# Wide input matmuls in a GRU, a new order of the opening, and a last attention batch whose logits follow head by head

## The chip, the core and the metric

The kernel runs on one core of one Trainium2 chip, in float32 throughout. The metric is the device time of one execution in microseconds. Engines are named as in the profile: PE is TensorE's matmul (PEld its weight load), DVE is VectorE, ACT is ScalarE, POOL is GpSimd, SP is SyncE, which issues most of the transfers.

## What is computed

`x` is (16, 256, 512) and `cond` is (16, 512). First an attention block with an adaptive norm is added to `x`, then a GRU runs over the 256 time steps of the result, with `cond` as its first state, and its states are added too.

```python
scale, shift = split(cond @ W_emb + b_emb)               # per batch
xn  = rms_norm(x, g_norm) * (1 + scale) + shift
q, k, v = heads(xn @ W_qkv)                              # 16 heads of 32
q, k = rms_norm(q, g_q), rms_norm(k, g_k)
o   = softmax(q k^T * 32**-0.5) v
x   = x + (o + o @ W_out)
# GRU over time, h = cond at t = 0
gi, gh = x_t @ W_ih + b_ih, h @ W_hh + b_hh
r, z = sigmoid(gi_r + gh_r), sigmoid(gi_z + gh_z)
n    = tanh(gi_n + r * gh_n)
h    = (1 - z) * n + z * h
out  = x + h
```

## The kernel before

**Attention.** The batches are worked one after the other. For each batch `project` (L246) makes q, k and v of two halves of 128 tokens in units of one half, one of q, k and v, and one of four chunks `k` of the contraction. `turn_qk` and `put_qk` bring q and k into `qT` and `kT`, with the heads on the partitions. The 16 heads are four groups of four. A group has its logits (`logits`, L314; four heads of 32 rows side by side in the array, one PSUM bank `lg0` to `lg3` each), their maxima (`maxima`, DVE, L330), exponentials with sums (`exps`, ACT, L336), a reciprocal (DVE, L344) and a scaling (`normalize`, POOL, L347). The weights are then turned by PE (`turn_pair`, L220, two heads at a time into two banks each), copied to SBUF (`put_turned_bank`, L376, DVE or ACT), multiplied with v (`weigh`, L393) and copied into `oT` (`put_weighed`, L404). `slot0` to `slot3` are the four groups of a batch. They mix the attention of batch b with the projections of batch b + 1, so PE has work while the other engines make the softmax. `last_batch` has no next batch to mix in: there the turn of a group stands in the slot of the group after it, and its `weigh` one slot later still.

**Opening.** The weights arrive while batch 0 is normed. `rows` holds `b_emb` and `g_norm`, and is turned into columns by PE. `g_q`, `g_k` and a second layout of `cond` (`rows_b`, `cond_p`) are loaded by SP after `x` of batch 1 and turned by PE just before q and k are turned (L674, L675). The biases of the GRU follow on SP (L129 to L131). `Stats` and `norm_qk` norm q and k from PSUM.

**GRU.** `h` is kept turned, hidden units on the partitions. A gate's PSUM tile has 32 partitions for each quarter of 128 units, 16 batches for each of two steps: a pair of steps shares its tiles, and two pairs alternate. Each product is four matmuls, one for each quarter, in four column tiles of the array. `gate_part` (L803) adds one chunk of the contraction. `input_part` adds the input's share for both steps of a pair at once, 128 columns for each of the gates r, n and z. `state_part` adds the state's share for one step. The tile of n has two blocks, the input's share and the state's, since r multiplies only the second. `open_gate` writes the biases by matmuls the first time, and `seed` by ACT copies later. In each step PE does the state's products (three gates, four chunks), then one step of `output_step` (`oT @ W_out` for a later block of 16 steps, 256 columns), then half of the next pair's input products (`parts[6 * s : 6 * s + 6]`). Meanwhile DVE turns the gates (`turned`, L827), ACT makes r, n and z, DVE makes h (L935 to L937), and POOL adds the result to `x`. `project_first` makes the `W_out` products of the first 16 steps within the last batch, chunk k from group k.

**Order.** Under `manual_schedule` the engines PE, DVE, ACT and POOL take their instructions in the written order. SP is not among them: its transfers go when their buffers are free and its queue comes to them.

Of the kernel before, what the change touches and what calls it, by code (L numbers as in the profile page):

```python
# [19 lines left out]
def kernel(  # L20
# [69 lines left out]

    rows = p1.tile([12, P], F32, tag="qkn", name="rows", bufs=4)
    nc.scalar.dma_start(rows[0:8, :], b_emb.rearrange("(m c) -> m c", c=P))
    nc.scalar.dma_start(rows[8:12, :], g_norm.rearrange("(m c) -> m c", c=P))
    x_tiles = {}
# [15 lines left out]
    rows_b = p1.tile([2, P], F32, tag="qkn", name="rows_b", bufs=4)  # L110
    cond_p = p1.tile([KC * B, P], F32, tag="qkn", name="cond_p", bufs=4)
    b_more = p1.tile([P, 2, P], F32, name="b_more")
    for r, g in ((0, g_q), (1, g_k)):
        nc.sync.dma_start(
            rows_b[r : r + 1, :].rearrange("o (i d) -> o i d", d=DH),
            g.rearrange("(o i d) -> o i d", o=1, i=1).to_broadcast([1, HG, DH]),
        )
    for k in range(KC):
        nc.sync.dma_start(
            cond_p[k * B : (k + 1) * B, :].rearrange("b (j c) -> b j c", c=32),  # L120
            cond.rearrange("b (j k c) -> k b j c", k=KC, c=32)[k],
        )
    for j in range(4):
        bi, bh = (
            b.rearrange("(o g j f) -> j o g f", o=1, g=3, f=P)[j].to_broadcast([32, 3, P])
            for b in (b_ih, b_hh)
        )
        r = slice(32 * j, 32 * j + 32)
        nc.sync.dma_start(b_rows[r, 0:3, :], bi)  # L129
        nc.sync.dma_start(b_rows[r, 3, :], bh[:, 2, :])  # L130
        nc.sync.dma_start(b_more[r], bh[:, 0:2, :])  # L131
# [172 lines left out]
    def logits(b, g):  # L304

        w = Group()
        w.b, w.g = b, g
        w.lg = [
            ps_lg.tile([P, NT, T], F32, tag=f"lg{i}", name=f"lg_{b}_{g}_{i}") for i in range(HG)
        ]  # L310
        for n in range(NT):
            for i in range(HG):
                r = slice(i * DH, (i + 1) * DH)
                nc.tensor.matmul(  # L314
                    w.lg[i][:, n, :],
                    qT[r, g, n * P : (n + 1) * P],
                    kT[r, g, :],
                    start=True,
                    stop=True,
                )  # L320
        w.turned = []
        w.neg = small.tile([P, HG, NT], F32, tag="neg", name=f"neg_{b}_{g}")
        w.den = small.tile([P, HG, NT], F32, tag="den", name=f"den_{b}_{g}")
        w.rden = small.tile([P, HG, NT], F32, tag="rden", name=f"rden_{b}_{g}")
        w.attn = [None] * HG
        return w

# [154 lines left out]
    def slot2(b, w, prev, st):  # L482
# [19 lines left out]
        if b == 0:  # L502

            for c in range(KC):
                d = wo[:, c, c * P : (c + 1) * P]
                nc.vector.tensor_tensor(d, d, ident, ALU.add)
        elif b == 1:
            nc.vector.tensor_tensor(b_rows[:, 0:2, :], b_rows[:, 0:2, :], b_more, ALU.add)
# [49 lines left out]

    def last_batch(prev):


        b, before = B - 1, None
        w = logits(b, 0)
        for g in range(NG):
            if before:
                weigh(before, "Z")
            turn_pair(prev, 0, "AX")
            maxima(w, (0, 1))
            exps(w, (0, 1))
            if before:  # L570
                put_weighed(before, nc.vector)
            turn_pair(prev, 1, "YZ")
            maxima(w, (2, 3))
            exps(w, (2, 3))
            put_turned_bank(prev, 0, nc.vector)
            normalize(w, (0, 1))
            put_turned_bank(prev, 2, nc.vector)
            put_turned_bank(prev, 1, nc.scalar)
            put_turned_bank(prev, 3, nc.scalar)
            if g < NG - 1:  # L580
                normalize(w, (2, 3))
                before, prev, w = prev, w, logits(b, g + 1)
        project_first(0)
# [3 lines left out]
        turn_pair(w, 0, ("lg2", "lg3"))  # L587
        turn_pair(w, 1, "AX")
        weigh(prev, "Z")
        put_turned(w, "vava")  # L590
        put_weighed(prev)
        weigh(w, "Y")
        put_weighed(w, nc.vector)
        project_first(2)
        project_first(3)

# [3 lines left out]
    with tc.manual_schedule(engines=ORDERED):  # L600
# [17 lines left out]
        tp = tile_ps("tp_rows", "A")  # L618
        nc.tensor.transpose(tp[:, :12], rows, ident[:12, :12])
        nc.vector.tensor_copy(cols[:, :12], tp[:, :12])  # L620
        for k in range(KC):
            for j in range(4):
# [9 lines left out]
        norm_apply(0, batches[0].rs.second())  # L632
        load_x(2)
# [19 lines left out]
        for k in range(KC):  # L653
            for n in range(NT):
                for i in range(2):
                    accs[n][i] = project(0, n, i, (k,), accs[n][i])
        v = project(0, 0, 2, range(KC), "lg0")
        norm_first(1)
        batches[1].rs.first()
        norm_apply(1, batches[1].rs.second())  # L660
        s0, s1 = Stats(0, 0), Stats(0, 1)
        s0.add(0, s0.square(0, accs[0][0]))
        s0.add(1, s0.square(1, accs[0][1]))
        sq = s1.square(0, accs[1][0])
        s0.rs.first()
        s1.add(0, sq)
        sq = s1.square(1, accs[1][1])
        rstd = s0.rs.second()
        s1.add(1, sq)
        s1.rs.first()  # L670
        qk0 = norm_qk(0, 0, accs[0], rstd)
        qk1 = norm_qk(0, 1, accs[1], s1.rs.second())
        tp = tile_ps("tp_rows_b", "lg1")
        nc.tensor.transpose(tp[:, :2], rows_b, ident[:2, :2])  # L674
        nc.tensor.transpose(tp[:, 64 : 64 + KC * B], cond_p, ident[: KC * B, : KC * B])  # L675
# [4 lines left out]
        norm_first(2)  # L680
        nc.vector.tensor_copy(cols[:, 12:], tp[:, :2])
        nc.vector.tensor_scalar(gq_col, cols[:, 12:13], DH ** -0.5, None, ALU.mult)
        nc.vector.tensor_copy(gk_col, cols[:, 13:14])
        nc.vector.tensor_copy(h0P.rearrange("p k b -> p (k b)"), tp[:, 64 : 64 + KC * B])
# [6 lines left out]
        for b in range(B - 1):  # L691
            for g in range(NG):
                w = logits(b, g)
                (slot0, slot1, slot2, slot3)[g](b, w, prev, st)
                prev = w
        last_batch(prev)

    TG = P // B  # L700
    xins = {}

    def in_blocks(a, i, j, s):

        a = a[:, i * TG : (i + 1) * TG, :].rearrange("b (s i) (j f) -> s j b i f", s=2, f=P)
        return a[s, j]

    def load_block(i):
        if i < T // TG:
            xins[i] = xin.tile([P, TG // 2, KC, 32], F32, tag="xin", name=f"xin_{i}")  # L710
            for j in range(4):
                for s in range(2):
                    r = 32 * j + B * s
                    nc.sync.dma_start(
                        xins[i][r : r + B].rearrange("b i q c -> b i (q c)"), in_blocks(x, i, j, s)
                    )

    for i in range(4):
        load_block(i)


    whh = wpool.tile([P, KC, 3 * D], F32, tag="w_b", name="whh")
    load_rows(whh, w_hh)
# [7 lines left out]

    R_, Z_, N_ = range(3)
    gates = [
        [tile_ps(f"g{name}_{i}", banks[i], (P, w, P)) for i in range(2)]
        for name, banks, w in (("r", ("A", "lg2"), 1), ("z", ("X", "lg3"), 1), ("n", "ZY", 2))
    ]
# [42 lines left out]
    def open_gate(p, g):  # L781

        for i in range(gates[g][p].shape[1]):
            for j in range(4):
                nc.tensor.matmul(
                    gates[g][p][32 * j : 32 * j + 32, i, :],
                    ident[:, 32 * j : 32 * j + 32],
                    b_rows[:, g + i, :],

                    start=(i == 0),  # L790
                    stop=True,
                    skip_group_check=True,
                )

    def seed(p):

        nc.scalar.copy(gates[R_][p % 2][:, 0, :], b_rows[:, 0, :])
        nc.scalar.copy(gates[N_][p % 2], b_rows[:, 2:4, :])
        nc.scalar.copy(gates[Z_][p % 2][:, 0, :], b_rows[:, 1, :])

    def gate_part(dst, rows, w, g, k, stationary):
        for j in range(4):
            nc.tensor.matmul(  # L803
                dst[32 * j : 32 * j + rows, :],
                stationary,
                w[:, k, g * D + P * j : g * D + P * j + P],
                start=False,
                stop=True,
                skip_group_check=True,
            )  # L810

    def input_part(p, g, k):
# [3 lines left out]
        gate_part(gates[g][p % 2][:, 0, :], 32, wih, g, k, x2)  # L816

    def state_part(t, g, hT):

        dst = gates[g][t // 2 % 2]  # L820
        for k in range(KC):
            gate_part(dst[:, dst.shape[1] - 1, :], hT.shape[2], whh, g, k, hT[:, k, :])
# [42 lines left out]
    with tc.manual_schedule(engines=ORDERED):  # L865
# [11 lines left out]
        for g in (R_, N_, Z_):  # L877
            open_gate(0, g)
            state_part(0, g, h0P)
            for k in range(KC):  # L880
                input_part(0, g, k)
        parts = [(g, k) for g in (R_, N_, Z_) for k in range(KC)]
# [104 lines left out]
```

## Time and profile before

| | us |
|---|---|
| median of 3 timed runs | 1752.92 (1748.24 to 1756.32) |
| profiled execution, its own time | 1767.2 |
| its span, first to last instruction | 1765.4 |
| opening, to the first logits | 0 to 35.79 |
| attention of batches 0 to 14 | 35.79 to 586.39 |
| last batch and the GRU's step 0 | 586.39 to 630.64 |
| GRU from step 1 | 630.64 to 1765.4 |

PE busy is 99% of the span, PEld 78%, DVE 60%, ACT 42%, POOL 18%. The mean granted clock of PE is 0.995. In a timeline row the figures are the start in us, the length of the merged stretch, the engine, the line, the operation, and the number of records (x32). Each float32 matmul shows as two records ("passes"), each with its own weight load. In a row of waits the figures are us in total, how often, and the longest. In a row of windows they are the stretch, its length, the busy time of PE, PEld, DVE, ACT and POOL, the granted clock (PEclk), the share of the DMA engines and GB/s.

### The profile page before, as it was taken

The page shows a single profiled execution, that of the slowest core. Times are in us where ns is not written, and L with a number is a line of the kernel's source. Part 1 is how long each engine was busy: PE and PEld are TensorE (multiplying, and loading weights), DVE is VectorE, ACT ScalarE, POOL GpSimd, SP SyncE. Part 2 cuts the span into 40 slices and gives each one's busy share as a digit, 9 for nine tenths or more (in the row PEclk, how much of TensorE's full clock was granted, in tenths as well). Part 3 has the DMA queues.
Part 4 walks back from the last instruction along what each step waited for, and adds up shares of the span by engine and source line. Part 5 has one row for each costly group of instructions (what it writes and reads, how often), then busy time and mean ns, then how long its engine had stood idle before and what let it go on. Part 6 is the DMA issues. An engine that isn't in the chain of part 4 may idle for free.

```text
span 1752.9 us, 103866 instructions
## 1 busy us (share of the span) xinstructions
PE 1734.2 (99%) x46980; PEld 1375.6 (78%) x46980; DVE 1055.3 (60%) x3313; ACT 740.9 (42%) x2694; POOL 315.6 (18%) x773
## 2 busy tenths in 40 slices
PE   8999999999999999999999999999999999999998
PEld 4444444444444589999999999999999999999997
DVE  4777777777776755555555555555555555555554
ACT  4777877787777722222222222222222222222222
POOL 0433444334433500000000000000000000000000
PEclk9999999999999999999999999999999999999999
DMA  7300000000000310000000100000001000000000
GB/s 247 78 14 14 14 26 14 14 14 14 14 2 2 74 28 22 17 17 23 23 17 16 23 23 17 17 23 23 17 17 22 23 17 17 17 10 11 11 17 16
DMA packets 49962, 44.90 MB, mean 26 GB/s; under 512 B 9619, under 2 KB 42751, under 8 KB 49519
## 3 DMA queue, kind: packets, MB, share of 16 engines
q1 hardware_dynamic: 49399, 38.21, 8.3%
q8 instruction: 368, 6.03, 1.5%
q14 instruction: 75, 0.61, 0.1%
q10 hardware_dynamic: 120, 0.04, 0.0%
HBM read 29.83 MB, written 8.39 MB: 22 GB/s over the span
## 4 chain that ended last, share of the span: by engine, by line
PE 97%; DVE 1%; ACT 1%; issue 1%; DMA 0%; SPq 0%; DVEq 0%; ACTq 0%
PE qkv L246 20%; PE gr L803 19%; PE gn L803 19%; PE gz L803 19%; PE o L747 6%; PE lg L314 4%; PE tpa L220 4%; PE o L393 4%; PE tpqk L220 1%; ACT attn L336 1%; PE tpx L220 1%; DMA we<-in_L_cond_W_emb_dram 0%; PE first L549 0%; DVE trh L827 0%; ACT n L908 0%
## 5 line engine op out<-in xcount | busy, mean ns | idle before, releaser
L246 PE MATMUL qkv<-wq,xnT 128*32 128x512 f32 x3072 | 355.6, 597 | 1.1 <-DVE xnT L238 1.1
L347 POOL TENSOR_SCALAR attn<-attn,rden 128x256 f32<-128x256 f32 x510 | 232.8, 478 | 378.3 <-DVE rden L344 254.2
L904 ACT ACTIVATE r<-trr 128x64 f32<-128x64 f32 x256 | 65.6, 256 | 521.1 <-DVE trr L827 521.1
L336 ACT ACTIVATE attn<-lg,neg 128x256 f32<-128x256 f32 x512 | 234.4, 483 | 64.0 <-DVE neg L330 46.9
L246 PEld LDWEIGHTS qkv<-wq,xnT 128*32 128x32 f32 x3072 | 88.3, 109 | 183.3 <-issue 158.2
L827 DVE STREAM_TRANSPOSE trr<-gr 128x128 f32<-128x128 f32 x256 | 81.1, 317 | 249.8 <-PE gr L803 249.7
L908 ACT ACTIVATE n<-n 128x64 f32<-128x64 f32 x256 | 65.7, 257 | 309.8 <-DVE n L907 306.9
L330 DVE TENSOR_REDUCE neg<-lg 128x2 f32<-128x512 f32 x256 | 159.2, 683 | 48.2 <-PE lg L314 48.1
L803 PE MATMUL gn<-wih,xT 128*32 128x128 f32 x4096 | 172.1, 273 | 0.1
L827 DVE STREAM_TRANSPOSE trh<-gn 128x128 f32<-128x128 f32 x256 | 81.1, 317 | 143.3 <-PE gn L803 143.3
L747 PE MATMUL o<-oT,wo 128*32 128x256 f32 x1920 | 159.9, 379 | 0.0
L803 PEld LDWEIGHTS gn<-wih,xT 128*32 128x32 f32 x4096 | 136.0, 110 | 12.7 <-issue 0.3
L803 PE MATMUL gr<-whh,padded 128*32 128x128 f32 x4096 | 141.8, 273 | 2.5 <-DVE padded L937 1.7
L803 PE MATMUL gr<-wih,xT 128*32 128x128 f32 x4096 | 142.8, 273 | 0.2
L803 PE MATMUL gz<-wih,xT 128*32 128x128 f32 x4096 | 142.6, 273 | 0.3
L803 PE MATMUL gz<-whh,padded 128*32 128x128 f32 x4096 | 142.1, 273 | 0.0
L803 PE MATMUL gn<-whh,padded 128*32 128x128 f32 x4096 | 141.6, 273 | 0.0
L803 PE MATMUL gr<-whh,h 128*16 128x128 f32 x4064 | 140.5, 273 | 0.4
L803 PE MATMUL gn<-whh,h 128*16 128x128 f32 x4064 | 140.4, 273 | 0.2
L803 PE MATMUL gz<-whh,h 128*16 128x128 f32 x4064 | 140.1, 273 | 0.0
L939 POOL TENSOR_TENSOR y<-xT,padded 128x64 f32<-128x64 f32 x128 | 41.1, 321 | 538.6 <-DVE padded L937 538.6
L803 PEld LDWEIGHTS gr<-wih,xT 128*32 128x32 f32 x4096 | 127.2, 110 | 13.0 <-issue 0.6
(127 smaller groups left out, 2782.0 us busy)
## 6 DMA issues: line engine op xcount, KB each, us to landing
x<-in_x_dram SPq DMA_DIRECT2D x16, 512.0 KB, 3.6
xin<-in_x_dram SPq DMA_DIRECT2D x256, 32.0 KB, 2.8
out_dram<-osb SPq DMA_DIRECT2D x248, 32.0 KB, 2.8
wq<-in_L_cond_W_qkv_dram SPq DMA_DIRECT2D x4, 768.0 KB, 9.9
wih<-in_L_cond_W_ih_dram SPq DMA_DIRECT2D x16, 192.0 KB, 7.0
whh<-in_L_cond_W_hh_dram SPq DMA_DIRECT2D x16, 192.0 KB, 6.7
we<-in_L_cond_W_emb_dram SPq DMA_DIRECT2D x4, 512.0 KB, 6.1
wo<-in_L_cond_W_out_dram SPq DMA_DIRECT2D x1, 1024.0 KB, 10.5
```

The lines of the kernel that those rows point to most:

```text
L220: nc.tensor.transpose(dst[r], src[q], ident[q, q])
L246: nc.tensor.matmul(a[32 * j : 32 * j + 32, :], batches[b].xnT[:, k, n * P + 32 * j : n * P + 32 * j + 32], wq[:, k, s * D : (s + 1) * D], ...
L314: nc.tensor.matmul(w.lg[i][:, n, :], qT[r, g, n * P : (n + 1) * P], kT[r, g, :], start=True, stop=True,)
L330: nc.vector.tensor_reduce(w.neg[:, i, :], w.lg[i], AX.X, ALU.max, negate=True)
L336: nc.scalar.activation(a[:, n, :], w.lg[i][:, n, :], AF.Exp, bias=w.neg[:, i, n : n + 1], accum_out=w.den[:, i, n : n + 1],)
L347: engine.tensor_scalar(w.attn[i][:, n, :], w.attn[i][:, n, :], w.rden[:, i, n : n + 1], 1.0, ALU.mult, ALU.mult,)
L393: nc.tensor.matmul(w.o[i * DH : (i + 1) * DH, :], v[:, k, h * DH : (h + 1) * DH], w.attnT[:, i, k, :], start=(k == 0), stop=(k == NT - 1),)
L747: nc.tensor.matmul(acc[32 * j : 32 * j + 32, :], w[:, k, P * j + 32 * m : P * j + 32 * m + 32], rhs, start=(k == 0), stop=(k == KC - 1),)
L803: nc.tensor.matmul(dst[32 * j : 32 * j + rows, :], stationary, w[:, k, g * D + P * j : g * D + P * j + P], start=False, stop=True, skip_gr ...
L827: nc.vector.transpose(tr.rearrange("p q s b -> p (q s b)"), gate)
L904: nc.scalar.activation(r, turned("r", t, gr[:, 0, :])[:, :, s, :], AF.Sigmoid)
L908: nc.scalar.activation(n, n, AF.Tanh)
```

## The change

It has three parts.

1. **GRU.** The tile of r gets a second block, and the input's share of n goes there. So `input_part` for r is one matmul of 256 columns (r's and n's columns of `W_ih`, two separated blocks of the moving operand) for each quarter and chunk, and z keeps 128 columns. The state's share of n has a tile to itself. `parts` has 8 entries in place of 12, three in the first step of a pair and five in the second. DVE turns the input's share of n after r, not before it. `open_gates` opens tiles with matmuls as wide as the tile.
2. **Opening.** `g_q` and `g_k` come with `rows` on ACT's queue. The units of q and k of batch 0 have a new order, and so have the statistics behind them. The biases and the first state move to `load_small`, issued in `slot2` of batch 0; the first state's second layout is copied from `h0T` by DMA.
3. **Last batch.** The logits of a head are written after the exponentials that free its bank, and its maximum follows them. A group is turned and weighed in one slot. `project_first(0)` moves into the last slot. The openings of step 0's gates and its state products stand between the last turns, `weigh` and `project_first(3)`.

The diff, cut to its core:

```diff
+    def load_small():
+        for j in range(4):
...
+            for i, g in enumerate((0, 2, 1)):
+                nc.sync.dma_start(b_rows[r, i, :], bi[:, g, :])
+            nc.sync.dma_start(b_rows[r, 3, :], bh[:, 2, :])
+            nc.sync.dma_start(b_more[r], bh[:, 0:2, :])
+            for q in range(KC):
+                nc.sync.dma_start(h0P[r, q, :], h0T[32 * q : 32 * q + 32, j, :])
...
+    def add_logits(w, heads):
+        for i in heads:
+            w.lg[i] = ps_lg.tile([P, NT, T], F32, tag=f"lg{i}", name=f"lg_{w.b}_{w.g}_{i}")
+        for n in range(NT):
+            for i in heads:
+                r = slice(i * DH, (i + 1) * DH)
+                nc.tensor.matmul(
+                    w.lg[i][:, n, :],
+                    qT[r, w.g, n * P : (n + 1) * P],
+                    kT[r, w.g, :],
...
-        elif b == 1:
-            nc.vector.tensor_tensor(b_rows[:, 0:2, :], b_rows[:, 0:2, :], b_more, ALU.add)
+            load_small()
+        elif b == 2:
+            for i in range(2):
+                a = b_rows[:, 2 * i, :]
+                nc.vector.tensor_tensor(a, a, b_more[:, i, :], ALU.add)
...
+    def open_gates(p, which=(R_, N_, Z_)):
+        for g, name, bank, row, n in (
+            (R_, "r", ("lg2", "A")[p], 0, 2), (N_, "n", ("lg3", "X")[p], 3, 1),
+            (Z_, "z", "ZY"[p], 2, 1),
+        ):
...
+    def gate_part(dst, rows, w, first, k, stationary):
+        for j in range(4):
+            nc.tensor.matmul(
+                dst[32 * j : 32 * j + rows],
+                stationary,
+                w[:, k, :].rearrange("p (g j c) -> p j g c", g=3, c=P)[:, j, first::2][:, : dst.shape[1]],
...
     def last_batch(prev):
-        b, before = B - 1, None
-        w = logits(b, 0)
+        w = logits(B - 1, 0)
+        maxima(w, range(HG))
         for g in range(NG):
-            if before:
-                weigh(before, "Z")
+            last = g == NG - 1
             turn_pair(prev, 0, "AX")
-            maxima(w, (0, 1))
             exps(w, (0, 1))
-            if before:
-                put_weighed(before, nc.vector)
+            put_turned_bank(prev, 0, nc.vector)
             turn_pair(prev, 1, "YZ")
-            maxima(w, (2, 3))
-            exps(w, (2, 3))
-            put_turned_bank(prev, 0, nc.vector)
+            put_turned_bank(prev, 2, nc.vector)
             normalize(w, (0, 1))
-            put_turned_bank(prev, 2, nc.vector)
             put_turned_bank(prev, 1, nc.scalar)
             put_turned_bank(prev, 3, nc.scalar)
-            if g < NG - 1:
-                normalize(w, (2, 3))
-                before, prev, w = prev, w, logits(b, g + 1)
-        project_first(0)
+            if last:
+                project_first(0)
+            else:
+                after = logits(B - 1, g + 1, ())
+                for i in (0, 1):
+                    add_logits(after, (i,))
+                    maxima(after, (i,))
+            weigh(prev, "Y")
+            exps(w, (2, 3))
+            put_weighed(prev, nc.vector)
+            if last:
+                break
+            normalize(w, (2, 3))
+            for i in (2, 3):
+                add_logits(after, (i,))
+                maxima(after, (i,))
+            prev, w = w, after
         project_first(1)
         normalize(w, (2,), nc.vector)
         normalize(w, (3,))
-        turn_pair(w, 0, ("lg2", "lg3"))
-        turn_pair(w, 1, "AX")
-        weigh(prev, "Z")
-        put_turned(w, "vava")
-        put_weighed(prev)
-        weigh(w, "Y")
+        turn_pair(w, 0, "AX")
+        put_turned_bank(w, 0, nc.vector)
+        put_turned_bank(w, 1, nc.scalar)
+        project_first(2)
+        turn_pair(w, 1, "YZ")
+        put_turned_bank(w, 2, nc.vector)
+        put_turned_bank(w, 3, nc.scalar)
+        open_gates(0, (R_, N_))
+        weigh(w, "A")
         put_weighed(w, nc.vector)
-        project_first(2)
+        open_gates(0, (Z_,))
+        state_part(0, R_, h0P)
         project_first(3)
+        state_part(0, N_, h0P)
+        state_part(0, Z_, h0P)
...
-        for k in range(KC):
-            for n in range(NT):
-                for i in range(2):
-                    accs[n][i] = project(0, n, i, (k,), accs[n][i])
+        for ks, n in (((0,), 0), ((0,), 1), ((1,), 0), ((1,), 1), ((2, 3), 0), ((2, 3), 1)):
+            for i in range(2):
+                accs[n][i] = project(0, n, i, ks, accs[n][i])
...
-        nc.scalar.copy(gates[R_][p % 2][:, 0, :], b_rows[:, 0, :])
-        nc.scalar.copy(gates[N_][p % 2], b_rows[:, 2:4, :])
-        nc.scalar.copy(gates[Z_][p % 2][:, 0, :], b_rows[:, 1, :])
+        nc.scalar.copy(gates[R_, p % 2], b_rows[:, 0:2, :])
+        nc.scalar.copy(gates[N_, p % 2][:, 0, :], b_rows[:, 3, :])
+        nc.scalar.copy(gates[Z_, p % 2][:, 0, :], b_rows[:, 2, :])
...
-        parts = [(g, k) for g in (R_, N_, Z_) for k in range(KC)]
+        parts = [(g, k) for g in (R_, Z_) for k in range(KC)]
...
-            if s == 0:
-                ni = turned("i", t, gn[:, 0, :])
...
             nc.scalar.activation(r, turned("r", t, gr[:, 0, :])[:, :, s, :], AF.Sigmoid)
+            if s == 0:
+                ni = turned("i", t, gr[:, 1, :])
...
-                for g, k in parts[6 * s : 6 * s + 6]:
+                for g, k in (parts[:3], parts[3:])[s]:
                     input_part(p + 1, g, k)
```

The blocks of x for the GRU and `W_hh` are now written before `last_batch` (the blocks first, as they were).

## The prediction

> **What bounds the kernel now.** I read the page first: shares, the chain that ended last, the groups; then the timeline of TensorE (PE) inside the second half, the waits there, and every engine's timeline of the two stretches that the diff reorders (0 to 60 us, 586 to 631 us).
>
> ```profile
> PE 1742.9 (99%) x46980; PEld 1384.4 (78%) x46980; DVE 1054.6 (60%) x3313; ACT 741.4 (42%) x2694; POOL 316.7 (18%) x773
> ...
> PE 96%; DVE 1%; ACT 1%; DMA 1%; issue 1%; SPq 0%; DVEq 0%; ACTq 0%
> ...
> L747 PE MATMUL o<-oT,wo 128*32 128x256 f32 x1920 | 169.9, 379 | 0.9 <-issue 0.8
> ```
>
> PE carries 96% of the chain, so only PE's passes and its stalls count, apart from the ends and the last attention batch. Two steps of the recurrence, in PE's timeline:
>
> ```profile
> 661.78 1.06 PE L803 MATMUL gr<-whh,h 128*16 128x128 f32 x32
> 662.65 1.06 PE L803 MATMUL gn<-whh,h 128*16 128x128 f32 x32
> 663.52 1.06 PE L803 MATMUL gz<-whh,h 128*16 128x128 f32 x32
> ...
> 666.14 1.06 PE L803 MATMUL gr<-whh,padded 128*32 128x128 f32 x32
> ```
>
> A step is 666.14 - 661.78 = 4.36 us. 32 passes take 0.87 us from start to start: eight rounds of four column tiles, 109.1 ns a round of 128 columns. A step has 24 rounds for the state, 12 for the input, two of 256 columns for the output: 36 x 0.1091 = 3.93, so a 256 round takes (4.362 - 3.93)/2 = 0.216 us. The step is PE's own streaming, nothing else. The last 16 steps (no output product) take 4.23 and 4.18 us, with PE waiting for h: that is the recurrence's own chain, 0.13 us below the step.
>
> But some steps are longer. What the weight loads (PEld) waited for in 640 to 1690 us, and two of the places:
>
> ```profile
> PEld gz L803 <- issue: 4.8, 15, 0.5
> PEld gn L803 <- issue: 3.4, 11, 0.3
> PEld o L747 <- issue: 2.8, 7, 0.5
> PEld gr L803 <- issue: 2.8, 8, 0.5
> ```
> ```profile
> 762.65 0.12 PEld L747 LDWEIGHTS o<-oT,wo 128*32 128x32 f32 x3 [0.53 <-issue]
> ```
>
> 13.8 us in 41 stops, waiting for no engine. They stand at 758.6, 762.65, 766.7 us: one block of instructions apart. Counting TensorE's records, every such stop falls on the same place modulo 256, some 1.4 us after a packet of the instruction queue ended (16 KB each). So the instruction stream is late: 304 instructions a step, 256 each 3.67 us.
>
> Last batch, granted clock (PEclk is the third figure from the end):
>
> ```profile
> 590.22:593.63 3.41, 2.87 (x22) 1.55 (x26) 1.99 (x6) 2.85 (x11) 2.82 (x7) 1.00 1.00 222
> 593.63:597.05 3.42, 3.42 (x46) 2.45 (x40) 2.78 (x5) 2.93 (x13) 0.84 (x2) 0.50 1.03 228
> ```
>
> Here PE has gaps, and the clock falls to half for 3.4 us, and again from 603.87 to 610.70.
>
> **The change, part by part.** Sums are against the profiled execution (1767.2 us, span 1765.4). The median of the timed runs, 1752.92, is 14.3 us lower, almost exactly all late fetches (14.2 us over the second half): timed runs must have few of them. I return to this at the end.
>
> *Opening.* Now q and k of batch 0 finish after 13 to 16 of 16 units of 0.86 us; in the new order after 10, 12, 14, 16. DVE's line of statistics starts 2.6 us earlier; the last unit ends where it did (28.7 us). Worked through: second sum of squares 29.7 to 30.35, scale 31.7, q and k of half 1 normalized 31.7 to 32.95 (now 32.33 to 33.62), no wait for gq_col (now 33.54 to 33.93), puts 33.0 to 34.6 (now 33.98 to 35.64). First logits at 34.75 instead of 35.79: -1.0. The value product, ending at 32.06, is then PE's bound. Moved past: SP loses 18 small DMAs (8.0 to 25.6 us), so x of batch 2, W_out and W_ih are issued earlier, behind W_qkv on one queue; nothing waits for them. ACT's queue gets two broadcasts (0.26 to 0.58 each); its first work is at 5.43, waiting for x: hidden. Without that cover 0.9. The 36 small DMAs of load_small take some 15 us of SP at 0.42 each, at about 70 us; x tiles are asked for a batch (36.6 us) ahead: nothing, or at worst one x late by some us. The copy from h0T has no row before; the nearest, small loads, land in 2 us, and it is needed 500 us later. The bias sum, one DVE operation of 0.43 us, becomes two, in a batch where PE is dense: nothing. W_hh, now written before the last batch, still waits for W_qkv's buffer (last read at 585.4), its transfers end near 600, and its first reader comes at 617: 17 us of cover.
>
> *Last batch.* Per group the chain now is: last exponential, logits, maxima, exponentials, copies; exponentials start at 588.34, 593.68, 599.58, 605.15. In the new order a head's logits follow its exponentials and maxima are ready. Cost: heads alone. [...] Row: four packed heads, 1.11 us; one head alone starts passes at +0, 0.32, 0.54, 0.75, so two pairs are 3.3 us. [...] By the trace today's heads also wait one by one (0.69 us each at 589.41, 590.32, 591.24), so the loss fills gaps; I take the timeline.
> New wait: DVE's copy of the weighed group stands ahead of the reciprocal of heads 2 and 3 and waits for weigh; behind it POOL's four scalings, then the next turn. The circle: copy and reciprocal 0.65, POOL 2.1, rest of the turn 0.45, logits of two heads 1.7, weigh 1.05: 5.9 us. PE's own work per group is 5.65. Exponentials start at 588.34, 593.05, 598.1, 603.9, the last end at 609.65 (now 610.04): -0.4 only.
> Tail: from there to step 1's state product (now 630.64). PE has W_out products 1 to 3, turns, weigh, gates, input, 3 output steps. Opened gates and the state products of step 0 (3.5 us) now fill waits that were idle (0.97 before the last weigh) or come before; half clock until 610.70 cost 0.9. Worked: turn at 611.8, weigh 616.05, last W_out product 618.1 to 619.8, input 621.6 to 624.2, step 1 at 627.65. ACT's table load (1.28) and the first step's chain end at 627.35, just hidden. Part: -3.0. Bounds: 0 to -4, and with the clock shut a loss (rival 2).
>
> *Wide input.* Per pair of steps eight times two rounds of 128 (0.218) become one of 256 (0.216): 2.4 ns each, 19.5 ns. 119 pairs: -2.3; the last eight pairs are bound by h. Two separated blocks as moving operand: nearest row, eight pieces of 32 (ps_emb), 384 ns against 379 for one piece: I take no cost. ACT's seeds 260 + 363 + 260 stay so in sum. The n transpose (0.31) moves between r's and h's; DVE idles 0.56 there for PE: hidden.
>
> *Fetch.* 608 instructions per pair become 544: 8 x 4 x 2 fewer. A block lasts 4.1 us instead of 3.67. [...] The trace shows stops of 0.27 (most) to 0.49 us: with 0.42 more per block nearly all go. In the profile -11 of 14.2. In timed runs: without stops this execution would be 1753.0, and the runs are 1748.2 to 1756.3, so they have perhaps 0 to 8; I take -3, with 0 and -11 as ends.
>
> Sum of the profiled run: 1.0 + 3.0 + 2.3 + 11 = 17.3, to 1749.9. Of the median: 1.0 + 3.0 + 2.3 + 3 = 9.3, to 1743.6.
>
> **Rivals.** (1) *Timed runs have no late fetches:* -6.3, 1746.6. For it: 1767.2 - 14.2 meets the median. Against: the runs' spread of 8 us. Or *they have as many as the profile:* -17.3, 1735.6; against it the same meeting.
> (2) *The clock shuts in the last batch.* Shut stretches followed windows in which PE was busy 2.87 of 3.41. The new order is denser (5.65 of 5.9), which speaks against, but single heads use a quarter of the array. PE is then the bound, so each shut window costs 1.7; five are 8.5: 1752.1, no gain.
> (3) *The moved n transpose lands on the chain.* If it delays h's transpose by its whole 0.317 us, the chain is 4.234 + 0.317 = 4.55, 0.19 over the step: x 119 = +22.5, with -7 from the rest: 1768.4, slower. It decides as soon as the delay exceeds 0.13 us. Against: the 0.56 us gap.
> (4) *The wide product isn't faster*, if rounds of 256 over split blocks take 0.218 or more: 1745.9, inside the first case.
>
> **How the numbers follow.** First case 0.45 (1739 to 1748, most of it the fetches' size); no fetch gain 0.20; full gain 0.20; clock 0.10; chain 0.05. The time is the first case's, 1743.5. The range takes in both ends of the fetches and the shut clock, 1734 to 1752; the chain is left out. 0.5% is 8.8 us, about what a measurement of this kernel can tell; it lies at 1744.1. Faster: half of the first case (0.24), a fifth of the second (0.04), all of the third: 0.48. Slower: the chain, 0.05. The rest, 0.47, within.
>
> **What would show it.** First logits near 34.8; exponentials of the last batch at 4.7 to 5.8 us distance and clock 1.00 from 597 on; step 1's state product some 4 us earlier; steps of 4.350 and 4.358; PEld's "issue" waits in the second half under 4 us; some 336 instruction packets (now 368). I am wrong if steps pass 4.37, if h's transpose waits for DVE, or if the late fetches stay with fewer instructions.

## The result and the profile after

| | before | after |
|---|---|---|
| timed, median | 1752.73 (1747.62 to 1756.32, 9 runs) | 1748.63 (1740.84 to 1751.17, 9 runs) |
| ratio | | 0.9967 (95%: 0.995 to 0.9984) |
| profiled execution, own time | 1767.2 | 1741.04 |
| first logits | 35.79 | 33.49 |
| attention of batches 0 to 14 | 550.60 | 550.74 |
| last batch, to step 1's state product | 44.25 | 39.67 |
| from there to the end | 1134.77 | 1115.35 |

The kernel is faster by 0.33%. The nine times of after are two groups: four at 1740.84 to 1742.05, with a mean granted clock of 0.998 to 1.000, and five at 1748.63 to 1751.17, at 0.990 to 0.993. The profiled execution is of the first group. So "after" is two numbers, and most of what follows asks what stands between them.

The page of after, with the lines that answer to those of before:

```profile
PE 1723.5 (99%) x42866; PEld 1274.8 (73%) x42866; DVE 1052.2 (60%) x3313; ACT 740.4 (43%) x2693; POOL 315.6 (18%) x773
...
q8 instruction: 336, 5.51, 1.3%
...
PE 94%; DVE 2%; DMA 2%; ACT 1%; issue 1%; POOL 0%; ACTq 0%; DVEq 0%; SPq 0%; POOLq 0%
...
L593 PE MATMUL gr<-wih,xT 128*32 128x256 f32 x4096 | 269.6, 379 | 0.0
```

PE is still the bound. The wide product of r and n takes 379 ns a record, what `o<-oT,wo` took with one unbroken block: the two separated blocks cost nothing that shows. The instruction queue brings 336 packets, not 368.

The steps of a pair, in PE's timeline of after:

```profile
654.49 1.12 PE L593 MATMUL gr<-whh,h 128*16 128x128 f32 x32
655.36 1.12 PE L593 MATMUL gn<-whh,h 128*16 128x128 f32 x32
656.23 1.12 PE L593 MATMUL gz<-whh,h 128*16 128x128 f32 x32
...
658.83 1.12 PE L593 MATMUL gr<-whh,padded 128*32 128x128 f32 x32
```

658.83 - 654.49 = 4.34 us. Over the steps that carry an output product the median is 4.347 and 4.357 us, where it was 4.362 twice: 20 ns a pair. The weight loads (PEld) have no wait for "issue" left in 640 to 1690 us. These are all their waits there:

```profile
PEld gr L593 <- DVE padded L951: 24.5, 113, 0.7
PEld gr L593 <- DVE h L951: 0.9, 3, 0.3
```

The loads wait earlier for `padded`, but PE itself idles no more for it: 2.9 us before all these products together, 2.5 in before.

In every trace the granted clock changes only at multiples of one length, 3.413 us, counted from any other change. The last batch of after in windows of that length, counted back from its change at 1737.7 us:

```profile
583.97:587.38 3.41, 3.01 (x57) 2.14 (x50) 1.99 (x4) 2.23 (x7) 2.49 (x6) 1.00 0.89 220
587.38:590.80 3.42, 3.42 (x27) 2.14 (x28) 3.40 (x7) 3.42 (x15) 1.55 (x4) 1.00 1.04 228
```

The clock is 1.00 throughout, and stays so until 1737.7 us. Exponentials start at 586.18, 590.74, 595.87 and 601.17.

### The profile page after: what moved, and what is told of

Its sections match the earlier page's. It is cut to its first block, busy times and chain, and to the rows that moved or that the text cites. A ratio compares the mean times of both kernels' runs of the same rounds, so it can differ in the third digit from the quotient of the medians.

```text
span 1749.7 us, 95655 instructions
## 1 busy us (share of the span) xinstructions
PE 1733.4 (99%) x42866; PEld 1276.8 (73%) x42866; DVE 1052.4 (60%) x3313; ACT 740.8 (42%) x2693; POOL 315.7 (18%) x773
## 4 chain that ended last, share of the span: by engine, by line
PE 94%; DMA 2%; DVE 2%; ACT 1%; issue 1%; SPq 0%; POOL 0%; DVEq 0%; ACTq 0%
PE gr L593 25%; PE gz L593 18%; PE qkv L244 18%; PE gn L593 13%; PE o L795 6%; PE lg L322 4%; PE tpa L218 4%; PE o L395 4%; PE tpqk L218 1%; DMA wih<-in_L_cond_W_ih_dram 1%; ACT attn L338 1%; PE tpx L218 0%; PE first L554 0%; DMA wq<-in_L_cond_W_qkv_dram 0%; DVE trh L844 0%
## 5 line engine op out<-in xcount | busy, mean ns | idle before, releaser
L593 PE MATMUL gr<-wih,xT 128*32 128x256 f32 x4096 | 269.6, 379 | 0.0
L593 PEld LDWEIGHTS gr<-wih,xT 128*32 128x32 f32 x4096 | 138.6, 110 | 79.6
L795 PE MATMUL o<-oT,wo 128*32 128x256 f32 x1920 | 148.9, 379 | 0.0
L593 PEld LDWEIGHTS gr<-whh,padded 128*32 128x32 f32 x4096 | 115.0, 109 | 30.3 <-DVE padded L951 28.9
L593 PE MATMUL gz<-wih,xT 128*32 128x128 f32 x4096 | 136.2, 273 | 0.0
L593 PE MATMUL gn<-whh,padded 128*32 128x128 f32 x4096 | 136.0, 273 | 0.0
L593 PE MATMUL gz<-whh,padded 128*32 128x128 f32 x4096 | 136.0, 273 | 0.0
L593 PE MATMUL gr<-whh,h 128*16 128x128 f32 x4064 | 135.1, 273 | 0.3
L593 PE MATMUL gn<-whh,h 128*16 128x128 f32 x4064 | 135.0, 273 | 0.0
L593 PEld LDWEIGHTS gz<-wih,xT 128*32 128x32 f32 x4096 | 118.7, 110 | 20.6
```

Of the source, the lines that this page charges most:

```text
L593: nc.tensor.matmul(dst[32 * j : 32 * j + rows], stationary, w[:, k, :].rearrange("p (g j c) -> p j g c", g=3, c=P)[:, j, first::2][:, : ds ...
L795: nc.tensor.matmul(acc[32 * j : 32 * j + 32, :], w[:, k, P * j + 32 * m : P * j + 32 * m + 32], rhs, start=(k == 0), stop=(k == KC - 1),)
```

## The experiments

After this result two theories stood. **A:** the change does what it says, and in half of the executions the granted clock falls to half within the last batch, since single heads use a quarter of the array's rows (records of 32*128, where a full one is 128*128); that eats most of the gain. **B:** the gain is small because timed runs of before have few late fetches; the clock is noise that both kernels share. "Before" below is the kernel before, timed beside the run on the same chip; a ratio is against it. A "shut" window is one at 0.50 granted clock.

**1. Both kernels again, nothing edited.**

> The changed kernel once more. Its nine runs fall into two groups, 1740.8 to 1742.1 us at a granted clock of 0.998 to 1.000 and 1748.6 to 1751.2 at 0.990 to 0.993. Theory (the clock gate shuts over most of the last batch in the second group: 0.008 x 1747 = 14 us of missing clock, some eight windows of 3.4 us at half): two groups again, 7 to 8 us apart, with nothing between, and the time follows the mean clock. Rival (late fetches make the spread): the times spread evenly and do not follow the clock.

> The kernel before once more, for its profile. Theory (the profiled execution's 14 us of late fetches were a rare case; the timed median of 1750.6 to 1752.7 has few): issue waits of PEld in the second half of 0 to 3 us, GRU part of 1119 to 1121 us against 1134.8. Rival (they are the rule): over 10 us.

Measured: after again 1745.69 (12 runs, ratio 0.9973, 0.9958 to 0.9988), six runs at 1740.94 to 1742.73 and six at 1748.65 to 1752.31. The profiled one is of the upper group. Before again 1749.72 (1748.36 to 1751.13; ratio 1.0007, 0.9997 to 1.0017), and its profile, 1750.43, has one "issue" row in the whole of 640 to 1690 us, where the first one had 13.8 us:

```profile
PEld gz L803 <- issue: 0.2, 1, 0.2
```

So of the two profiled executions of before only one had late fetches to speak of. The windows of after again show where its 9.3 us went:

```profile
586.86:590.27 3.41, 3.02 (x43) 2.43 (x40) 3.34 (x6) 2.62 (x11) 1.15 (x3) 1.00 1.02 234
590.27:593.68 3.41, 3.41 (x23) 1.41 (x23) 2.20 (x6) 3.41 (x16) 1.85 (x4) 0.50 1.02 217
593.68:597.10 3.42, 3.42 (x42) 2.57 (x38) 2.02 (x6) 1.19 (x6) 1.85 (x4) 0.50 1.05 223
...
610.75:614.16 3.41, 3.41 (x48) 2.46 (x52) 2.64 (x5) 2.08 (x7) 1.29 (x4) 0.50 0.01 2
614.16:617.57 3.41, 3.41 (x68) 1.80 (x60) 1.25 (x5) 0.93 (x5) 1.19 (x3) 1.00 0.02 5
```

Seven windows, 23.9 us, at half clock. The last batch takes 47.40 us instead of 39.67: +7.73. A shut window at 13.4 us makes the opening 1.45 longer, and the rest is equal: GRU 1115.38 against 1115.35. The medians of the two groups stand 7.9 us apart in the first nine runs and 9.2 in these twelve. Before again loses four windows there (589.6 to 596.4, 603.2 to 610.1) and takes 45.56. In PE's timeline of after again, the window ahead of the first fall holds one gap, before the first single head:

```profile
588.78 2.46 PE L322 MATMUL lg<-kT,qT 32*128 32x256 f32 x8 [0.38 <-ACT attn L338]
```

But the profiled after, whose clock stayed up, has the same gap, and the same busy time (3.01 of 3.41) in the window that holds it:

```profile
587.25 2.04 PE L322 MATMUL lg<-kT,qT 32*128 32x256 f32 x8 [0.40 <-ACT attn L338]
```

So neither gap nor busy time decides alone.

**2. The wide product undone.** `gate_part` writes two products of 128 columns; tiles, order and all else as in after.

```diff
+        for i in range(dst.shape[1]):
             for j in range(4):
                 nc.tensor.matmul(
-                    dst[32 * j : 32 * j + rows],
+                    dst[32 * j : 32 * j + rows, i : i + 1],
...
-                    w[...][:, j, first::2][:, : dst.shape[1]],
+                    w[...][:, j, first::2][:, i : i + 1],
```

> The changed kernel, but the input's product for r and n goes out as two matmuls of 128 columns, so 304 instructions a step again. Theory (fewer instructions end the late fetches): steps go back to 4.36 us (+2.3 us in sum) and PEld's issue waits in the second half come back, some 5 to 14 us; 1744 to 1757 timed against the changed kernel's 1748.6, at the least 2.3 more at the same granted clock. Rival (the late fetches came from something else in that one execution, or the opening's and last batch's shift): no more than +2.3 us, and no issue waits.

Measured: 1753.59 (12 runs; ratio 1.001, 0.9996 to 1.0024): three runs at 1744.47 to 1746.25, nine at 1753.02 to 1756.24. By their medians the groups lie 4.6 and 3.7 us above those of after again, on the same chip. Its profile has the GRU at 1119.82 us, +4.47 against after. Steps are 4.362 again: 20 ns x 119 pairs = 2.4. The rest is late steps. Counted as what each step takes beyond the median of its kind, over 235 steps, they cost 4.03 us here and 2.02 in after. The weight loads' "issue" waits came back with 1.4 us only, not the 5 to 14 expected.

**3. The last batch undone.** `last_batch` in the old order, all else as in after.

> The changed kernel with the old last batch (loop, order of weigh and turn, and gates opened after the last W_out product). Theory (the timed runs lose the last batch's gain to the clock gate, which shuts in some runs of the new order): the profile's last batch is 3 to 5 us longer than the changed kernel's 39.7 us, yet the timed median is within 3 us of 1748.6, and the spread of the granted clock over the runs is smaller than the changed kernel's 0.990 to 1.000. Rival (the last batch keeps its gain in all runs): the median is 3 to 5 us higher, 1752 to 1754.

Measured: 1745.61 (1743.73 to 1748.65, 9 runs; ratio 0.9975, 0.9966 to 0.9985), without two groups. The last batch takes 47.05 us with five shut windows, 7.4 more than in after and not the 3 to 5 expected. The median is that of after again on the same chip (1745.69), so in the timed median the new last batch brought nothing.

**4. The opening's order undone.** The order of units and statistics of before; g_q and g_k still early.

> The changed kernel with the old order of batch 0's q and k units and of the statistics behind them; the loads stay in the new order. Theory (the order is worth about 1 us, the other 1.3 of the opening's 2.3 us came from the clock, which was at half from 13.4 to 16.8 us in the profile of before and full in that of the changed kernel): first logits 1 us later than 33.5, at 34.5, when the clock is open. Rival (the loads' order gave the gain): first logits at 33.5 as in the changed kernel.

Measured: 1742.3 (1739.94 to 1751.78, 12 runs; ratio 0.9964, 0.9951 to 0.9977), eight runs at 1742.61 or less and four at 1747.28 to 1751.78. In the profile the first logits come at 36.60 us, with two shut windows at 10.5 us, so this profile can't tell the order from the clock. The median below after's is the draw of the groups, and the GRU's 1113.64 us (see the end); no run shows a gain by the old order.

**5. Both undone**, so that the wide product and the early loads are left.

> The changed kernel with both the old last batch and the old order of batch 0's units and statistics: what is left of the change is the wide input product and the order of the small loads. Theory (the order of the opening is worth 1 us, the wide product and its fetches 4): 1745.6 + 1 = 1746.6, 4 us under the kernel before. Rival (the opening is worth nothing, since e3's runs at an open clock match the changed kernel's): 1745.6.

Measured: 1744.46 (1742.12 to 1745.99, 9 runs; ratio 0.9976, 0.9967 to 0.9986). First logits at 33.72 with the clock open until then; last batch 42.86 with two shut windows; GRU 1113.65. The median lies under both expected cases. So the wide product and the early loads alone reach the ratio that the whole change has (0.9967 and 0.9973): in the timed median the two new orders add nothing.

**6. Single heads over all 128 rows.** `r = slice(i * DH, (i + 1) * DH) if len(heads) > 1 else slice(0, P)` in `add_logits`.

> The changed kernel, but a head's logits that go out alone use all 128 rows of q and k (four heads summed: another result, the same instructions and times but for the little overlap of neighbouring heads, +0.2 us a pair). Theory A (the gate shuts and stays shut because single heads use 32 of 128 rows): no shut windows in the last batch, all runs at 1741 to 1743. Theory B (the gate follows PE's idle time, whose gap at the batch's start is untouched, and where the free windows lie): two groups 8 us apart as in the changed kernel.

Measured: 1742.88 (8 runs; ratio 0.9972, 0.9962 to 0.9982): six at 1742.48 to 1743.25, two at 1746.02 and 1746.39, none above. The last batch takes 41.13 us, +1.46, and no window shuts.

**7. Logits in pairs of heads,** so that two row groups (64 of 128 rows) are in use: `add_logits(after, (0, 1))` and `(2, 3)`, maxima likewise.

> The changed kernel with the logits of heads 0 and 1, and of 2 and 3, issued as a pair in two row groups instead of one head after the other: 4 rounds a pair instead of 7, no later than now for head 3. If PE is the bound of the last batch when the clock is shut (rival 2 of the prediction), the shut case loses its 8 us: 9 rounds x 0.43 less over three groups, 3 to 7 us faster, and the open case 1 to 2 us by the circle over POOL. Median 1739 to 1744. If the shut case is not bound by PE's rounds: two groups as now, 1741 and 1749.

Measured: 1748.81 (12 runs; ratio 0.9988, 0.9974 to 1.0001), five at 1741.08 to 1741.87, seven at 1748.81 to 1750.29. With half of the rows the two groups remain (no run of the upper one was profiled). With the clock open nothing moved at all: last batch 39.72, exponentials at 586.19, 590.75, 595.90, 601.22. So single heads were not what the groups of heads waited for.

**8. All 128 rows, with the kernel's own result; and less POOL in the circle.** Three tiles of zeros take batch 15's q, each head in its own rows, so the other heads' k meets zeros. They lie in buffers that are free by then. A second kernel also has head 2 scaled by DVE; a third has only that.

```diff
+    def masked_fill():
+        for g in range(1, NG):
+            for i in range(HG):
+                r = slice(i * DH, (i + 1) * DH)
+                nc.sync.dma_start(qz[g][r, i, :], qT[r, g, :])
...
-                    qT[r, w.g, n * P : (n + 1) * P],
-                    kT[r, w.g, :],
+                    qz[w.g][:, i, n * P : (n + 1) * P] if alone else qT[r, w.g, n * P : (n + 1) * P],
+                    kT[:, w.g, :] if alone else kT[r, w.g, :],
...
-            normalize(w, (2, 3))
+            normalize(w, (2,), nc.vector)
+            normalize(w, (3,))
```

> A head's logits alone run over all 128 rows, with a copy of q in which the other three heads are zero (12 small transfers of 32 partitions after batch 15's q is ready); the result is the kernel's own. If it is the quarter of the array that shuts the clock: no shut window in the last batch, last batch 41.1 us as in the run with full rows (it was 41.13 there, 39.67 with quarter rows), at most 2 us more if the transfers come late; timed runs 1742 to 1745, none at 1748 or above. If the gate goes by gaps or by chance alone: two groups again, 1742 and 1749, about half and half.

> As the kernel with zeroed rows, and head 2 of groups 0 to 2 of the last batch is scaled by DVE, head 3 by POOL, so POOL's share of the circle is 0.92 us in place of 1.84. If the circle of a group goes from the exponentials over the reciprocal and POOL to the second turn: 0.5 to 0.9 us less in each of three groups, last batch 1.5 to 2.8 us shorter than with zeroed rows alone. If it goes over weigh and the logits: the same time, within 0.3 us.

> The changed kernel with head 2 of groups 0 to 2 of the last batch scaled by DVE and head 3 by POOL, nothing else. With the clock open, if the circle goes over POOL: exponentials 4.2 to 4.8 us apart, where the changed kernel has 4.56, 5.13 and 5.30, and the last batch 37 to 38.2 us, not 39.67; runs of the upper group 1738.5 to 1740 where it had 1741. If it goes over weigh and the logits: 39.5 to 39.8 and 1741. If the clock shuts as often as before, half of the runs stay near 1748.

| | timed | ratio (95%) | last batch, profile |
|---|---|---|---|
| zeroed rows | 1744.53 (1744.47 to 1746.37, 10 runs) | 0.9976 (0.9967 to 0.9986) | 41.11, none shut |
| zeroed rows, head 2 on DVE | 1742.73 (1740.76 to 1743.40, 5 runs) | 0.9959 (0.9947 to 0.9972) | 40.90, none shut |
| head 2 on DVE alone | 1747.07 (1738.70 to 1750.53, 11 runs) | 0.9987 (0.9973 to 1.0001) | 47.41, seven shut |

The same stretch in the kernel with zeroed rows, gap included, runs on at full clock:

```profile
586.49:589.90 3.41, 3.03 (x28) 1.94 (x28) 3.41 (x8) 3.41 (x15) 0.73 (x2) 1.00 0.16 43
589.90:593.32 3.42, 3.42 (x48) 2.59 (x40) 2.94 (x6) 3.17 (x14) 2.96 (x7) 1.00 0.53 144
593.32:596.73 3.41, 3.41 (x30) 2.26 (x27) 2.61 (x6) 3.39 (x15) 1.85 (x4) 1.00 1.06 229
```

Its transfers come later (DMA share 0.16 and 0.53 against 1.02), but the kernel of experiment 6 has 1.00 and 1.01 there and stayed open too, so they are not needed for it. Of all runs with 128 rows (8 + 10 + 5) none is more than 3.9 us above the fastest of its kernel. With 32 rows (after, after again, head 2 on DVE) 20 of 32 are over 7 us above it, 33 of 56 with the wide product and the opening's order undone. So full rows take the long shut stretch away: no window shut in the last batch of their three profiles, seven in three of the five with 32 rows. They also make PE busy without a wait: eight records of single logits last 1.99 us, and 1.14 with 32 rows when their banks are free. The two weren't separated for the fall; for staying shut, busy time isn't it, since in after again PE was busy 3.42 of 3.42 us from 593.68 and the clock stayed at half.

What makes one execution with 32 rows shut and the next not? The grid of 3.413 us lies differently in each execution, and the five profiles with 32 rows sort by it. In the three that shut, the window that holds the gap begins 1.10, 1.20 and 1.35 us after batch 15's first logits (after again, wide undone, head 2 on DVE), and ends with 1.5 to 1.7 us of single heads (588.78 to 590.27 in after again). In the two that stayed open it begins 0.26 and 0.05 us before them (after, 583.97 against 584.23; opening's order undone), and has 0.1 and 0.3 us of single heads. In experiment 6 it began 1.53 us after them, with 3.03 us busy, and with all rows the clock stayed up. Idle time alone does not explain it: in after again PE is busy for 3.02 of 3.41 us (88%) or more in each of the ten windows from 583.44 to 617.57 us, the 3.02 in the one ahead of the fall, and in after no fall followed the one with 3.01.

An estimate from the records fits better than busy time: count the columns that each record moves by its share of 128 x 128, the largest shape in the records (rows times columns). A dense window of the GRU then holds some 4,040. From 35 to 1,720 us, in all 13 profiles, the ten windows at full clock ahead of a fall hold 660 to 1,450, and every other window at full clock holds 1,630 or more; the window with the gap has 1,420 in after again, 2,350 in after, 2,760 in experiment 6. In the opening and at the end it fails (770 at 7.2 us with head 2 on DVE alone, and no fall), so it points at how much of the array is used, and is no rule.

POOL's expectation failed. With zeroed rows, DVE's help moved the last batch from 41.11 to 40.90, not by 1.5 us. PE's timeline of that kernel says why:

```profile
596.02 1.99 PE L323 MATMUL lg<-kT,qz 128*128 128x256 f32 x8
597.95 1.21 PE L218 MATMUL tpa<-ident,attn 64*128 64x64 f32 x32
599.09 1.99 PE L323 MATMUL lg<-kT,qz 128*128 128x256 f32 x8
601.01 1.07 PE L396 MATMUL o<-attnT,v 128*32 128x256 f32 x16
```

Starts follow each other without a gap, 5.99 us a group: PE is the bound there. In after the same four rows are

```profile
595.51 1.67 PE L322 MATMUL lg<-kT,qT 32*128 32x256 f32 x8
597.11 1.71 PE L218 MATMUL tpa<-ident,attn 64*128 64x64 f32 x32
598.75 1.14 PE L322 MATMUL lg<-kT,qT 32*128 32x256 f32 x8
599.81 1.07 PE L395 MATMUL o<-attnT,v 128*32 128x256 f32 x16
```

with 5.31 us a group (595.51 to 600.82, where the next logits start). The turn is stretched from 1.21 to 1.71: its weight loads wait 0.33 and 0.25 us for POOL's scaling. The first logits are stretched from 1.14 to 1.67: theirs wait 0.41 for the exponentials that free the banks. No wait is longer than that, so speeding up one engine should give little. The two runs of the third kernel with the clock open, 1738.70 and 1738.73, are 2.3 us under after's 1741.0; some 1.9 of that is the GRU's late steps (2.02 us in after, 0.11 in that kernel's profile), 0.4 is left for POOL. No open run of it was profiled, so this split is an estimate.

**What the last batch costs, by its shut windows,** one row per profile:

| order, kernel | shut windows in it | last batch |
|---|---|---|
| old: both undone | 2 | 42.86 |
| old: before, first profile | 3 | 44.25 |
| old: before again | 4 | 45.56 |
| old: last batch undone | 5 | 47.05 |
| new: after; opening's order undone; pairs | 0 | 39.67; 39.73; 39.72 |
| new: after again; wide undone; head 2 on DVE | 7 | 47.40; 47.44; 47.41 |

The old order lies on a line: (47.05 - 42.86) / 3 = 1.40 us a window. Continued to no window, which no run showed, it gives about 40.1 us. The new order pays 7.73 / 7 = 1.10 a window. So with the clock fully open the two orders differ by perhaps 0.4 us. The new order's real effect is that its profiles have either no shut window or seven, where the four of the old order have two to five. That it always has them is not shown: two of the 33 runs of before timed beside experiments 1 to 4 have a mean clock of 0.999, so one shut window at most (0.0015 x 1747 us, at 1.71 us a window, is 1.5, the end's included).

**The best version** is the one with zeroed rows and head 2 on DVE: 1742.73, against 1748.88 for before on the same chip (0.9959), with all five runs at a clock of 0.997 or more. Its interval overlaps that of after, so it is not shown to beat after as measured there (0.9967); that it has no group at 1749 is what the runs show. Of the 3.71 us between its profile and that of the zeroed rows alone, 3.38 are in the GRU (1117.26 to 1113.88), which the edit does not touch, so DVE's share of the scaling is not what made it the best.

## Why the prediction came out as it did

The time lies inside the range, 5 us above the predicted 1743.5, and the sign is right. The gain is 4.1 us, not 9.3. Step by step:

- **Opening, -1.0.** About right in size. The first profile of before has a shut window at 13.4 us. After again has the same one and its first logits at 34.94, so -0.85, at the predicted place (34.75). With no such window in either it is 34.03 against 33.49, -0.54. With the old order and the early loads it is 33.72, but profiles of the new order with an open clock reach from 33.32 to 33.60, so the order is worth 0.1 to 0.4 us, and which of the two parts is larger is not shown. The shut window itself costs 1.45 (34.94 - 33.49), more than the edit brings.
- **Last batch, -3.0.** Too small by 1.6 us even against the profile that it was taken from (44.25 to 39.67 is -4.58). The worked times give 41.26 us to step 1 (627.65 - 586.39). Of the 1.6, the distances of the exponentials are 0.6: worked as 4.71, 5.05 and 5.8, measured 4.56, 5.13 and 5.30. The circle of 5.9 us a group, over weigh, DVE's copy and single logits, was too long, and the pairs of heads moved nothing, though PE was busy 2.81 us with them from 586.8 to 590.2 where after has 3.00. The last group's exponentials are 0.3, the tail 0.7: 17.3 us from the last exponential (606.6) to step 1 (623.90), 18.0 predicted. And the base's clock was undervalued: half clock until 610.70 was put at 0.9 us. By the table those two windows cost 2 x 1.40 = 2.8, and the one at 593.63 another 1.4. Measured against before again, with four, -5.9 with the clock open, and +1.8 with it shut.
- **Wide input, -2.3.** 20 ns a pair, 19.5 predicted. Right. Undoing it alone costs 4.47 us, the rest being late fetches.
- **Fetch, -11 of 14.2 in the profile, -3 in timed runs.** In the profile no "issue" row remains, as the first half says, but before again, with the old number of instructions, has only 0.2 us of it, so this is no proof that fewer instructions did it. (The stops of the first profile are 0.20 to 0.53 us, not 0.27 to 0.49; 36 of 41 are shorter than the 0.42 gained per block.) The second half was too much. From before again to after the late steps fall from 2.31 to 2.02 us, from the wide product undone to after from 4.03 to 2.02: -0.3 to -2. That lies between the first case and rival 1, nearer to the rival.
- **Rival 1, no late fetches, 1746.6:** near the truth on the fetches, but not what set the time.
- **Rival 2, the shut clock, chance 0.10.** This one decided the size. Five windows at 1.7 were to be 8.5 us; it was seven at 1.10, 7.7, in five of nine runs by their mean clock. The working had what it took ("single heads use a quarter of the array") and set it aside because PE would be denser. Density did not protect it: PE was busy some 3.02 of 3.41 us in the window with the gap, in open and shut executions alike, and full rows took the shut windows away (none in the last batch of three profiles). The failed step is that chance; that the range took the case in is what kept the time inside it.
- **Rival 3, the n transpose on the chain:** excluded. Steps got shorter, not 0.19 longer, and the transpose of the state's share still waits for PE, as the page of after has it:

```profile
L844 DVE STREAM_TRANSPOSE trh<-gn 128x128 f32<-128x128 f32 x256 | 81.1, 317 | 116.8 <-PE gn L593 116.8
```

- **Rival 4, wide not faster:** excluded by 379 ns a record and the steps.

The account from before again (four shut windows) to the profiled after (none): opening -0.54, attention +0.20, last batch -5.89, GRU -3.16, sum -9.39 (1750.43 to 1741.04). That it meets the predicted -9.3 of the median is luck: the last batch gave more, opening and fetches less. In timed runs it holds for four of nine. The other five lose 7.9 again (1748.9 - 1741.0), which leaves about -1.5 there, and the median of nine falls among them. That the measured gain is 4.1 and not 1.5 comes from its base: before had a median of 1752.73 in that measurement and 1748.9 to 1750.6 in the three later ones. Why is not shown.

## What to carry to other kernels

Before costing a new order of a stretch, read the granted clock there in more than one execution: at 1.1 to 1.4 us for each shut window of 3.41, five windows outweigh an edit that saves a few microseconds. Heads that are computed alone use 32 of the array's 128 rows (records of 32*128 against 128*128), and in this kernel full rows with zeros, 1.4 us dearer while the clock is open (41.11 against 39.67), were the steadier choice. A profile with a rare disturbance (13.8 us of late fetches) is a poor base for the sum: take the base from an execution near the median, and when the times of a kernel fall into two groups, explain the groups, not the median.

## What the runs showed that was not expected

- The clock shut for 23.9 us behind a window with no PE gap longer than 0.4 us and 88% busy time.
- Small late steps recur at a fixed distance in the GRU. In after one step in 32 (every 139.5 us, at 846.4, 986.0 and so on to 1544.1) is 0.23 us longer. DVE's timeline in a usual step and in such a one:

```profile
762.57 0.22 DVE L949 TENSOR_TENSOR padded<-h,n 128x64 f32<-128x64 f32 x1 [0.17 <-ACT n L923]
...
850.13 0.23 DVE L949 TENSOR_TENSOR padded<-h,n 128x64 f32<-128x64 f32 x1 [0.52 <-ACT z L925]
```

  ACT's n had started 0.36 us before the first (762.21) and 0.71 before the second (849.42), and DVE's own work before it ended at 849.62, so DVE was late with all its inputs there. Over the 235 steps this is 2.02 us in after, 3.82 with zeroed rows, 0.33 with zeroed rows and one more reciprocal on DVE in each group, 0.45 with the old opening. That changes far from the GRU move 1 to 3 us of it is measured; what lies behind the fixed period is not shown.
